# Moving layer 1's closing sums over neighbours beside other small matmuls, and layer 3's loads, in a four-layer graph network

## The chip, the cores and the metric

The kernel runs on one core of a Trainium2 chip. The metric is the device time of one launch in microseconds (us), as the median of several runs. A profile of one further execution gives the order of work on each engine: TensorE (PE, matmuls; PEld is its weight load), VectorE (DVE), ScalarE (ACT), GpSimd (POOL), and SyncE (SP), which here only issues transfers (DMAs).

## The reference

The input is 128 graphs of 64 nodes with 512 features each, an adjacency matrix of 64x64 for each graph, and the weights of four layers. Each layer normalises x over its features, takes the positive part h, and adds a graph operation on h to x. All numbers are 32-bit floats.

```
x = x + softmax_nodes(s * sum(q * (adj @ k)))[:, :, None] * v      # layer 0: q,k,v = h @ W
w = adj * exp(q @ k^T);  x = x + (w / sum(w)) @ v                  # layer 1
x = x + Wo(softmax(scores * 2 adj) @ v)                            # layer 2: 8 heads of 64
a = adj * exp(leaky_relu(sj + si + ab));  t = a / sum(a)           # layer 3
x = x + relu(h@Wk0 + t @ (h@Wk1) + t @ (t @ (h@Wk2)) + biases)
```

## The kernel before

**Tiling.** The 8192 nodes are cut into 32 blocks of 256 (`n_blk` = 32), each of them two groups of 128 rows (`TT` = 2), with two graphs to a group. The large products (512x512 weights) are written by `Product` as seven half-size products of a Strassen-like scheme: `first` and `second` make four of them, `late` the other three, and a `store` helper collects the results from PSUM with ACT, DVE and POOL. `side_by_side` runs the products of two weights together: first and second of part 0, first and second of part 1, late of part 0, late of part 1. It takes three lists of further actions, `between`: list 0 runs after the first part's `first`, list 1 before the late products of part 0, list 2 before those of part 1.

**Small tiles.** Products within a graph have only 64 rows and use a quarter or half of the matrix array. They are: `neighbour_sums` (L390, matmul on L397, 64x64 tiles of the array with 512 columns; its output is called pa in layer 0 and po in layers 1 and 3), den (L601, L861, row sums, one column), `products` (L375, matmul on L382, 128x64 tiles, output sc) and layer 2's scores and context (L665, L731). All other matmuls use the full 128x128 array.

**Order of layers.** Layers 0 and 1 go over pairs of blocks: `steps` (L915) is layer 0 of blocks 0 and 1, layer 1 of blocks 0 and 1, layer 0 of blocks 2 and 3, and so on. Layer 1 of a block ends with `layer1` computing sc and the weights e (L588 to L593). Its end, `layer1_end` (L595: den, po, the division, the addition to x on DVE, and the store of x to DRAM on L613), is put off: the loop keeps it in `open_end` and appends it to list 1 of the next step's `between`, ahead of the late products of that step's first part. Layer 0's end (`layer0_end`, L546, with the matmul sm_w) is put off to list 0 of the next step. `prepare` (L919) loads and normalises the next step's block in list 0, `turned` (L925) transposes it in list 2 (matmul tr, L195). The last end, of block 31, runs in layer 2's first block (L1027).

Layer 2 follows with loads three blocks ahead (`fetch2`), additions and norm in `prepare2` (L935), `layer2_in`, scores, values and context. The output product's `add_to` (L338) collects into x on DVE and POOL and names its last DVE instruction `taken` (L345); `keep_ab` (L281) names its DVE sum `kept` (L286). Layer 3 begins inside layer 2's last blocks: after block 29 and 30 of layer 2 come load, norm and `layer3_dots` (L802, four dot products hu on DVE, L810) of layer 3's blocks 0 and 1. Then `layer3_step(b)` does one block each: `layer3_head` with `begin` (L1003: load and norm of block b+2), the end of block b-1 (`layer3_end`: po, the output and its store on L910), the start of block b+1 (`layer3_in`: sm_i and the transposes); then `layer3_tail`, and last the dots of block b+2.

**Buffers.** PSUM is shared by three pools: `ps_tr` (2 banks, tag tr), `ps_mm` (4 banks, tag mm, two for each `Product`) and `ps_sc` (2 banks, tag sc). A tile has to wait until the earlier user of its bank is done. x has four buffers (`load_x`, L56), used by all layers; adjT has three; h has six.

**What sets the order.** Each engine works through its instructions one after the other. Their order on an engine is settled when the program is built: earlier source lines have precedence, and an instruction from further down is put ahead when the builder takes its inputs to be ready sooner. `tc.issue_after(ins)` holds the instructions of its block that are on the engine of `ins` behind `ins` in that engine's order; it adds no wait for `ins` to finish, and leaves other engines alone. Transfers of x, adjT and outputs are all issued by SP, in SP's order.

Of the kernel before, what the change touches and what calls it, by code (L numbers as in the profile page):

```python
# [13 lines left out]
P = 128  # L14
N = 64
D = 512
# [9 lines left out]
def kernel(ctx: ExitStack, tc: tile.TileContext, a: dict, out: bass.AP):  # L26
# [29 lines left out]
    def load_x(b: int, source, stage: int):  # L56
        x = big.tile([P, TT, D], FP, tag="x", name=f"x{stage}_{b}", bufs=4)
        nc.sync.dma_start(x, tokens(source))
        return x

    def load_adjT(b: int, stage: int):
        adjT = med.tile([P, TT, N], FP, tag="adjT", name=f"adjT{stage}_{b}")
        nc.sync.dma_start(adjT, tokens(adjT_d[rows(b), :]))
        return adjT
# [438 lines left out]
        yield m, u, c1, d, w1v, w2  # L503


    def layer0(b: int, x, adjT, hs, hT, between):
        ops = sums(hT, f"0_{b}")
        gv = big.tile([P, 2, TT, D], FP, tag="qk", name=f"gv_{b}")
        am = small.tile([P, TT, N], FP, tag="am", name=f"am_{b}", bufs=2)
        with tc.issue_after(behind_norm[0][0].ins):  # L510
            nc.gpsimd.tensor_tensor(
                am,
                adjT,
                mcol[:, b * TT : (b + 1) * TT].unsqueeze(2).to_broadcast([P, TT, N]),
                ALU.mult,
            )
        pa = [ps_tr.tile([P, D], FP, tag="tr", name=f"pa_{b}_{t}") for t in range(TT)]
        aggs = [
            med.tile([P, D], FP, tag="agg", name=f"agg_{b}_{t}", bufs=2) for t in range(TT)
        ]  # L520
        for t, to, at in neighbour_sums(pa, am, hs):
            nc.scalar.copy(aggs[t][to], pa[t][at])

        parts = [
            (ops, m0, None, lambda p: p.store(gv[:, 0]), f"g0_{b}"),
            (ops, w0v, None, lambda p: p.store(gv[:, 1]), f"v0_{b}"),
        ]
        side_by_side(*parts[:: 1 if b else -1], between=between)
# [15 lines left out]
        return x, gv, w, wd  # L544
# [21 lines left out]
                x[:, t, :], gv[:, 1, t, :], att[:, t : t + 1], x[:, t, :], ALU.mult, ALU.add  # L566
            )

    def layer1(b: int, x, adjT, hs, hT, between):

        m1, u1, c1, d1, w1v = made1[:5]
        ops = sums(hT, f"1_{b}")
        gT = big.tile([P, K, T], FP, tag="qk", name=f"gT_{b}")
        v = big.tile([P, TT, D], FP, tag="v", name=f"v1_{b}")
        _, of_v = side_by_side(
            (ops, m1, u1, lambda p: p.store_T(gT, u1), f"g1_{b}"),
            (ops, w1v, None, lambda p: p.store(v), f"v1_{b}"),
            between=between,
        )
        be = small.tile([P, TT], FP, tag="be", name=f"be_{b}")  # L580
        for t in range(TT):
            hc = med.tile([P, D], FP, tag="agg", name=f"hc_{b}_{t}", bufs=2)
            with tc.issue_after(of_v.kept.ins):
                nc.vector.scalar_tensor_tensor(
                    hc, hs[t], 1.0, c1, ALU.mult, ALU.mult, accum_out=be[:, t : t + 1]
                )
        nc.vector.tensor_scalar(be, be, d1, None, ALU.add)
        s = products(gT, hT, f"1_{b}")  # L588
        e = small.tile([P, TT, N], FP, tag="e", name=f"e1_{b}")
        for t in range(TT):  # L590
            nc.scalar.activation(e[:, t, :], s[:, t, :], AF.Exp, bias=be[:, t : t + 1])
        nc.vector.tensor_tensor(e, e, adjT, ALU.mult)
        return v, e  # L593

    def layer1_end(b: int, x, v, e, to):  # L595

        po = [ps_sc.tile([P, D], FP, tag="sc", name=f"po1_{b}_{t}") for t in range(TT)]
        den = [ps_tr.tile([P, 1], FP, tag="tr", name=f"den1_{b}_{t}") for t in range(TT)]
        for t in range(TT):
            for g in range(2):  # L600
                nc.tensor.matmul(  # L601
                    den[t][half[g ^ t]], e[half[g], t, :], ones_bd[half[g], g * N : g * N + 1],
                    start=True, stop=True,
                )
        parts = neighbour_sums(po, e, [v[:, t, :] for t in range(TT)])
        r = small.tile([P, TT], FP, tag="r1", name=f"r1_{b}")
        for t in range(TT):
            nc.vector.reciprocal(r[:, t : t + 1], den[t])
        for t, out_at, at in parts:
            nc.vector.scalar_tensor_tensor(  # L610
                x[out_at, t, :], po[t][at], r[at, t : t + 1], x[out_at, t, :], ALU.mult, ALU.add
            )
        nc.sync.dma_start(tokens(to), x)  # L613
# [180 lines left out]
                nc.gpsimd.tensor_tensor(bs, bs, bi, ALU.add)  # L794
        return us, c3, bs

    def layer3_norm(b: int, source):
        x = load_x(b, source, 3)
        adjT = load_adjT(b, 3)
        return x, adjT, norm(x, f"3_{b}")  # L800

    def layer3_dots(b: int, x, adjT, hs):  # L802
# [132 lines left out]
    def prepare2(b: int):  # L935
        if b < n_blk:
# [3 lines left out]
                nc.vector.tensor_tensor(x[:, t, :], x[:, t, :], b1v, ALU.add)  # L940
            normed2[b] = norm(x, f"2_{b}")

    def turned2(b: int):
        if b < n_blk:
            normed2[b] = transposed(normed2[b], f"2_{b}")
# [7 lines left out]
    loaded[1] = load_x(1, x_d[rows(1), :], 0), load_adjT(1, 0)  # L953
    setup = setup1()
    next(setup)
    open_end = []
    for i, (layer, b) in enumerate(steps):
        if i == len(steps) - 2:
            fetch2(0)
        between = [[], [chore], []]  # L960
        if i == 0:
            for n in (1, 2):
                between[n].append(lambda: next(setup))
        if i == 1:
            open_end.clear()
            made1 = next(setup)
        for n, end in open_end:
            between[n].append(end)
        if i + 1 < len(steps):
            between[0].append(lambda: prepare(i + 1))  # L970
            between[2].append(lambda: turned(i + 1))
        else:
            fetch2(1)
            between[0].append(lambda: prepare2(0))
            between[2].append(lambda: turned2(0))
        if layer == 0:
            softmax = layer0(b, *loaded[b], *normed[i], between)
            open_end = [(0, lambda b=b, softmax=softmax: layer0_end(b, *softmax))]
        else:
            attention = layer1(b, *loaded[b], *normed[i], between)  # L980
            open_end = [
                (1, lambda b=b, a=attention: layer1_end(b, loaded[b][0], *a, x1[b]))
            ]
            if b == n_blk - 2:
                open_end.append((1, lambda: fetch2(2)))
        if i == len(steps) - 3:
            made2 = setup2()

# [6 lines left out]
    def layer3_step(b: int, ahead: bool = True):  # L995

        nonlocal normed3
        x, al, ops = made_in.pop(0)  # L1000
        stages = layer3_in(b + 1, *normed3, made_in) if b + 1 < n_blk else iter(())

        def begin():  # L1003
            nonlocal normed3
            if b + 2 < n_blk and ahead:
                normed3 = layer3_norm(b + 2, x2[b + 2])

        y = layer3_head(b, ops, [
            [begin], [ending.pop()], [lambda: next(stages, None), lambda: next(stages, None)]
        ])  # L1010
        yield
        tail = layer3_tail(b, al, ops, y)
        for _ in range(2):
            next(tail)
            yield
        r, y0, kept = next(tail)
        ending.append(lambda: layer3_end(b, x, al, y, r, y0))
        if b + 2 < n_blk:
            with tc.issue_after(kept.ins):
                if ahead:  # L1020
                    normed3 = layer3_dots(b + 2, *normed3)
                else:
                    normed3 = layer3_norm(b + 2, x2[b + 2])
        yield

    qk, ops = layer2_in(0, normed2[0], [
        [lambda: prepare2(1), chore], [*(end for _, end in open_end), chore], [lambda: turned2(1)]  # L1027
    ])
    coming = values(0, ops)
    next(coming)  # L1030
# [8 lines left out]
    for b in range(n_blk):  # L1039
# [43 lines left out]
        if b == n_blk - 4:  # L1083
            made3 = setup3()
        if n_blk - 3 <= b < n_blk - 1:
            normed3 = layer3_dots(
                b - n_blk + 3, *layer3_norm(b - n_blk + 3, x2[b - n_blk + 3])
            )
        elif b == n_blk - 1:
            with tc.issue_after(of_o.taken.ins):  # L1090
                normed3 = layer3_dots(2, *normed3)


    for b in range(1, n_blk):
# [66 lines left out]
```

## Time and profile before

| | |
|---|---|
| median of 3 runs | 2647.34 us (2646.83 to 2647.69) |
| profiled execution: its own time | 2645.07 us |
| profiled execution: span from first to last instruction | 2643.3 us |
| granted TensorE clock, mean | 0.999 |
| TensorE busy | 2624.6 us (99%), 20752 matmuls |
| VectorE busy | 1695.9 us (64%) |
| GpSimd busy | 1292.8 us (49%) |
| ScalarE busy | 950.4 us (36%) |
| den of layer 1 (L601) | 256 matmuls 64x64, 9.3 us |
| po of layer 1 (L397) | 256 matmuls 64x64, 34.2 us |
| sc of layer 1 (L382) | 1024 matmuls 128x64, 36.9 us |
| pa of layer 0 (L397) | 256 matmuls 64x64, 35.9 us |

How to read it: "busy" is the time in which an engine had at least one instruction of the program in work; matmuls overlap in the array, so their durations add up to more than the time they take. In a line such as `L397 PE MATMUL po<-v,e 64*64 64x512 f32 x8`, L397 is the line of the kernel (that of a helper where a helper writes the instruction), `po<-v,e` says what is written from what, `64*64` is the part of the array that is used, and x8 counts instructions. In lines of time the first number is the start in us from the start of the span, the second the duration. "idle before <-X" is idle time of the engine and what ended it. In the view of waits the three numbers are total us, number of waits, and the longest. The chain of work runs back from the last instruction: at each step to what released it.

Layers 0 and 1 take roughly the first 1010 us of the span, layer 2 goes to about 1945 us, layer 3 to the end.

### The profile page before, as it was taken

The page shows a single profiled execution, that of the slowest core. Times are in us where ns is not written, and L with a number is a line of the kernel's source. Part 1 is how long each engine was busy: PE and PEld are TensorE (multiplying, and loading weights), DVE is VectorE, ACT ScalarE, POOL GpSimd, SP SyncE. Part 2 cuts the span into 40 slices and gives each one's busy share as a digit, 9 for nine tenths or more (in the row PEclk, how much of TensorE's full clock was granted, in tenths as well). Part 3 has the DMA queues.
Part 4 walks back from the last instruction along what each step waited for, and adds up shares of the span by engine and source line. Part 5 has one row for each costly group of instructions (what it writes and reads, how often), then busy time and mean ns, then how long its engine had stood idle before and what let it go on. Part 6 is the DMA issues. An engine that isn't in the chain of part 4 may idle for free.

```text
span 2643.3 us, 52749 instructions
## 1 busy us (share of the span) xinstructions
PE 2624.6 (99%) x20752; PEld 2250.6 (85%) x20752; DVE 1695.9 (64%) x4396; ACT 950.4 (36%) x2292; POOL 1292.8 (49%) x1585
## 2 busy tenths in 40 slices
PE   9999999999999999999999999999999999999998
PEld 5888888888888889999999999999877777777776
DVE  5676666666666676556556656656656666666665
ACT  3333343333333343333333333333333333333332
POOL 4443333333433335655655655655565555555554
PEclk9999999999999999999999999999999999999999
DMA  5111111111111122111111111111211111111110
GB/s 179 48 35 35 35 36 37 46 39 43 43 35 35 35 67 79 39 51 40 37 53 38 39 53 37 39 48 42 74 51 52 51 52 52 52 52 51 52 50 32
DMA packets 103200, 129.80 MB, mean 49 GB/s; under 512 B 40870, under 2 KB 50086, under 8 KB 102952
## 3 DMA queue, kind: packets, MB, share of 16 engines
q1 hardware_dynamic: 102376, 125.38, 14.3%
q8 instruction: 163, 2.67, 0.4%
q10 hardware_dynamic: 576, 1.05, 0.1%
q14 instruction: 85, 0.70, 0.1%
HBM read 76.07 MB, written 50.34 MB: 48 GB/s over the span
## 4 chain that ended last, share of the span: by engine, by line
PE 93%; DVE 2%; DMA 2%; POOL 1%; ACT 1%; issue 0%; SPq 0%; ACTq 0%; POOLq 0%; DVEq 0%
PE ab_v L256 12%; PE ab_y L256 11%; PE dc_v L256 9%; PE dc_y L256 8%; PE ab_g L249 4%; PE ab_k L249 4%; PE ab_g L256 4%; PE ab_q L249 4%; PE tr L195 4%; PE ab_o L256 4%; PE dc_g L249 3%; PE dc_g L256 3%; PE po L397 3%; PE dc_k L249 3%; PE dc_q L249 3%; PE dc_o L256 3%
## 5 line engine op out<-in xcount | busy, mean ns | idle before, releaser
L184 ACT ACTIVATE h<-x,nmr,rstd 128x512 f32<-128x512 f32 x256 | 194.4, 806 | 239.8 <-DVE nmr L176 239.8
L174 POOL TENSOR_TENSOR rstd<-ve,neghalf 128x2 f32<-128x2 f32 x128 | 89.6, 700 | 373.8 <-DVE ve L172 373.8
L169 DVE BATCH_NORM_STATS2 stats<-x 128x6 f32<-128x512 f32 x256 | 165.5, 677 | 92.8 <-DMA x<-x 86.7
L256 PE MATMUL ab_y<-L_Wk,hT 128*128 128x256 f32 x768 | 203.9, 388 | 0.1
L256 PE MATMUL ab_v<-L_Wv,hT 128*128 128x256 f32 x768 | 200.8, 384 | 0.4 <-ACT qk L328 0.4
L256 PE MATMUL dc_v<-L_Wv,S 128*128 128x256 f32 x768 | 197.3, 380 | 0.0
L256 PE MATMUL ab_y<-L_Wk,S 128*128 128x256 f32 x768 | 197.2, 379 | 0.0
L256 PE MATMUL ab_v<-L_Wv,S 128*128 128x256 f32 x768 | 197.2, 379 | 0.0
L256 PE MATMUL dc_y<-L_Wk,S 128*128 128x256 f32 x768 | 193.8, 381 | 3.2 <-DVE u_y L882 3.1
L256 PEld LDWEIGHTS ab_y<-L_Wk,hT 128*128 128x128 f32 x768 | 137.3, 190 | 67.5 <-issue 25.2
L256 PEld LDWEIGHTS dc_y<-L_Wk,S 128*128 128x128 f32 x768 | 144.8, 190 | 26.6 <-DVE u_y L882 7.0
L256 PEld LDWEIGHTS ab_v<-L_Wv,S 128*128 128x128 f32 x768 | 146.1, 190 | 19.7
L256 PEld LDWEIGHTS ab_y<-L_Wk,S 128*128 128x128 f32 x768 | 146.1, 190 | 19.7
L256 PEld LDWEIGHTS dc_v<-L_Wv,S 128*128 128x128 f32 x768 | 143.6, 190 | 18.7 <-issue 0.8
L903 POOL TENSOR_TENSOR tz<-tz,y 128x512 f32<-128x512 f32 x63 | 91.3, 1450 | 126.0 <-ACT tz L900 125.9
L256 PEld LDWEIGHTS ab_v<-L_Wv,hT 128*128 128x128 f32 x768 | 136.0, 190 | 16.0 <-ACT qk L328 0.7
L195 PE MATMUL tr<-ident,h 128*128 128x128 f32 x1024 | 133.9, 274 | 0.0
L195 PEld LDWEIGHTS tr<-ident,h 128*128 128x128 f32 x1024 | 118.4, 142 | 7.3
L221 POOL TENSOR_TENSOR S<-hT 128x256 f32<-128x256 f32 x128 | 100.4, 784 | 34.0 <-ACT hT L198 33.6
L224 POOL TENSOR_TENSOR S<-hT 128x256 f32<-128x256 f32 x128 | 107.9, 843 | 7.1 <-DVE hT L200 7.1
L904 DVE SCALAR_TENSOR_TENSOR x<-tz,x 128x512 f32<-128x512 f32 x64 | 44.3, 692 | 102.6 <-POOL tz L903 102.6
L311 POOL TENSOR_TENSOR gv<-u_g,p_g 128x256 f32<-128x256 f32 x32 | 23.3, 729 | 173.0 <-DVE u_g L308 173.0
(238 smaller groups left out, 6474.6 us busy)
## 6 DMA issues: line engine op xcount, KB each, us to landing
x<-x SPq DMA_DIRECT2D x128, 512.0 KB, 3.5
x<-in_x_dram SPq DMA_DIRECT2D x32, 512.0 KB, 3.5
out_dram<-x SPq DMA_DIRECT2D x31, 512.0 KB, 2.8
adjT<-in_adjT_dram SPq DMA_DIRECT2D x64, 64.0 KB, 1.9
adjq<-in_adj_dram SPq DMA_DIRECT2D x64, 64.0 KB, 2.3
L_Wk<-in_L_Wk_dram SPq DMA_DIRECT2D x16, 256.0 KB, 5.5
L_Wv<-in_L_Wv_dram SPq DMA_DIRECT2D x12, 256.0 KB, 4.9
q<-in_L_Wqk_dram ACTq DMA_DIRECT2D x4, 256.0 KB, 5.3
```

What stands on the lines that cost most here:

```text
L169: nc.vector.bn_stats(stats[:, t, :], x[:, t, :])
L174: by_rows = nc.gpsimd.tensor_tensor(rstd, ve, neghalf, ALU.pow)
L184: nc.scalar.activation(h, x[:, t, :], AF.Relu, bias=nmr[:, t : t + 1], scale=rstd[:, t : t + 1])
L195: nc.tensor.transpose(pt[:, k, :], h[:, k * P : (k + 1) * P], ident)
L221: nc.gpsimd.tensor_tensor(S1, A21, A22, ALU.add)
L224: behind[0] = nc.gpsimd.tensor_tensor(S3, A11, A21, ALU.subtract)
L249: nc.tensor.matmul(dst[:, m * P : (m + 1) * P], w[:, place, k, m * P : (m + 1) * P], left[:, k, :], start=key not in self.begun, stop=last ...
L256: nc.tensor.matmul(dst, left[:, k, :], w[:, place, k, :], start=key not in self.begun, stop=last and k == 1, skip_group_check=True,)
L311: nc.gpsimd.tensor_tensor(y[:, 1, F:], self.u3, self.p5, ALU.add)
L397: nc.tensor.matmul(ps[t][half[g ^ t]], e[half[g], t, :], us[t][half[g]], start=True, stop=True)
L903: nc.gpsimd.tensor_tensor(tz[t], tz[t], y0[:, t, :], ALU.add)
L904: nc.vector.scalar_tensor_tensor(x[:, t, :], tz[t], 0.0, x[:, t, :], ALU.max, ALU.add)
```

## The change

Three things change.

1. `layer1_end` of block b no longer goes into a `between` list of the following step. The loop keeps it as the function `open_end`, and `layer0` and `layer1` take it as a new argument `before`, which they call only for odd blocks: `layer1` directly ahead of `products`, `layer0` directly ahead of its `neighbour_sums` (pa). So the end of an even block b runs in layer 1 of block b+1 ahead of sc, and the end of an odd block b in layer 0 of block b+2 ahead of pa. That of block 31 stays where it was. `fetch2(2)` goes along with the end of block 30. To make room, po of layer 1 moves from `ps_sc` to `ps_tr`, den from `ps_tr` to `ps_mm` (for block 31 to `ps_sc`), and pa from `ps_tr` to `ps_sc` (for even blocks one of its two tiles to `ps_mm`; block 0 stays).
2. Layer 3's load of x and adjT is split from its norm into `fetch3`. In `layer3_step(b)` the load of block b+3 is issued at the end of the step, after the dots of b+2; the norm of b+3 stays in `begin` of step b+1.
3. Two parts are tied: `prepare2(0)` behind `kept` of the value product of layer 1's block 30 (`first2`), and `layer3_dots` of blocks 0 and 1 behind `taken` of layer 2's output product.

```diff
-    def layer0(b: int, x, adjT, hs, hT, between):
+    def layer0(b: int, x, adjT, hs, hT, between, before):
...
-        pa = [ps_tr.tile([P, D], FP, tag="tr", name=f"pa_{b}_{t}") for t in range(TT)]
+        before()
+        pa = [
+            pool.tile([P, D], FP, tag=tag, name=f"pa_{b}_{t}")
+            for t, (pool, tag) in enumerate((
+                ((ps_sc, "sc"), (ps_sc if b % 2 else ps_mm, "sc" if b % 2 else "mm"))
+                if b else ((ps_tr, "tr"),) * 2
+            ))
+        ]
...
-    def layer1(b: int, x, adjT, hs, hT, between):
+    def layer1(b: int, x, adjT, hs, hT, between, before):
...
         nc.vector.tensor_scalar(be, be, d1, None, ALU.add)
+        before()
         s = products(gT, hT, f"1_{b}")
...
-        return v, e
+        return of_v, v, e
...
-        po = [ps_sc.tile([P, D], FP, tag="sc", name=f"po1_{b}_{t}") for t in range(TT)]
-        den = [ps_tr.tile([P, 1], FP, tag="tr", name=f"den1_{b}_{t}") for t in range(TT)]
+        po = [ps_tr.tile([P, D], FP, tag="tr", name=f"po1_{b}_{t}") for t in range(TT)]
+        pool, tag = (ps_mm, "mm") if b + 1 < n_blk else (ps_sc, "sc")
+        den = [pool.tile([P, 1], FP, tag=tag, name=f"den1_{b}_{t}") for t in range(TT)]
...
-    def layer3_norm(b: int, source):
-        x = load_x(b, source, 3)
-        adjT = load_adjT(b, 3)
+    loaded3 = {}
+
+    def fetch3(b: int):
+        if b < n_blk:
+            loaded3[b] = load_x(b, x2[b], 3), load_adjT(b, 3)
+
+    def layer3_norm(b: int):
+        x, adjT = loaded3.pop(b)
         return x, adjT, norm(x, f"3_{b}")
...
+    def first2(of_v):
+        with tc.issue_after(of_v.kept.ins):
+            prepare2(0)
+
...
-        for n, end in open_end:
+        for n, end in begun:
             between[n].append(end)
+        begun = []
...
-            between[0].append(lambda: prepare2(0))
+            between[0].append(lambda: first2(of_v))
...
-            softmax = layer0(b, *loaded[b], *normed[i], between)
-            open_end = [(0, lambda b=b, softmax=softmax: layer0_end(b, *softmax))]
+            softmax = layer0(b, *loaded[b], *normed[i], between, open_end if b % 2 else nothing)
+            begun = [(0, lambda b=b, softmax=softmax: layer0_end(b, *softmax))]
         else:
-            attention = layer1(b, *loaded[b], *normed[i], between)
-            open_end = [
-                (1, lambda b=b, a=attention: layer1_end(b, loaded[b][0], *a, x1[b]))
-            ]
-            if b == n_blk - 2:
-                open_end.append((1, lambda: fetch2(2)))
+            of_v, *attention = layer1(
+                b, *loaded[b], *normed[i], between, open_end if b % 2 else nothing
+            )
+
+            def open_end(b=b, a=attention):
+                layer1_end(b, loaded[b][0], *a, x1[b])
+                if b == n_blk - 2:
+                    fetch2(2)
+
...
             if b + 2 < n_blk and ahead:
-                normed3 = layer3_norm(b + 2, x2[b + 2])
+                normed3 = layer3_norm(b + 2)
...
                 if ahead:
                     normed3 = layer3_dots(b + 2, *normed3)
+                    fetch3(b + 3)
                 else:
-                    normed3 = layer3_norm(b + 2, x2[b + 2])
+                    fetch3(b + 2)
+                    normed3 = layer3_norm(b + 2)
...
-            normed3 = layer3_dots(
-                b - n_blk + 3, *layer3_norm(b - n_blk + 3, x2[b - n_blk + 3])
-            )
+            fetch3(b - n_blk + 3)
+            normed3 = layer3_norm(b - n_blk + 3)
+            with tc.issue_after(of_o.taken.ins):
+                normed3 = layer3_dots(b - n_blk + 3, *normed3)
         elif b == n_blk - 1:
             with tc.issue_after(of_o.taken.ins):
                 normed3 = layer3_dots(2, *normed3)
+            fetch3(3)
```

More of the change, by code (lines that the diff above doesn't have):

```diff
@@ L955, with nothing @@
     next(setup)
-    open_end = []
+    begun = []
+    def nothing():
+        pass
+    open_end = nothing
     for i, (layer, b) in enumerate(steps):
@@ L964 @@
         if i == 1:
-            open_end.clear()
+            begun = []
             made1 = next(setup)
-        for n, end in open_end:
+        for n, end in begun:
             between[n].append(end)
+        begun = []
         if i + 1 < len(steps):
@@ L1021, in layer3_step @@
                     normed3 = layer3_dots(b + 2, *normed3)
+                    fetch3(b + 3)
                 else:
-                    normed3 = layer3_norm(b + 2, x2[b + 2])
+                    fetch3(b + 2)
+                    normed3 = layer3_norm(b + 2)
         yield
     qk, ops = layer2_in(0, normed2[0], [
-        [lambda: prepare2(1), chore], [*(end for _, end in open_end), chore], [lambda: turned2(1)]
+        [lambda: prepare2(1), chore], [open_end, chore], [lambda: turned2(1)]
     ])
```

## The prediction, made before the changed kernel was run

> **What bounds the kernel now.** I read the page first (busy times, slices, chain), then the waits of the matrix engine, then the order of time around the moved work, then the chain inside one block of layer 3.
>
> ```profile
> PE 2624.6 (99%) x20752; PEld 2250.6 (85%) x20752; DVE 1695.9 (64%) x4396; ACT 950.4 (36%) x2292; POOL 1292.8 (49%) x1585
> PE 93%; DVE 2%; DMA 2%; POOL 1%; ACT 1%; issue 0%; SPq 0%; ACTq 0%; POOLq 0%; DVEq 0%
> ```
>
> TensorE (PE) is busy 99% of the span and is 93% of the chain that ended last. So time is won only by giving PE fewer or denser instructions, or by ending its few waits:
>
> ```profile
> PE tw_q L424 <- DMA q<-in_L_Wqk_dram: 5.7, 3, 5.1
> PE dc_y L256 <- DVE u_y L882: 3.1, 4, 1.1
> PE ab_o L256 <- DVE u_o L286: 1.5, 1, 1.5
> ```
>
> The first is the start of the kernel and isn't touched. The others lie in layers 2 and 3. Waits are small, so the denser question is what PE does between its matmuls. PE in order of time, in an odd block of layer 1 (start, duration, what):
>
> ```profile
> 516.95 1.03 PE L256 MATMUL dc_v<-L_Wv,hT 128*128 128x256 f32 x4
> 517.91 0.29 PE L601 MATMUL den<-ones_bd,e 64*64 64x1 f32 x8
> 518.05 1.07 PE L397 MATMUL po<-v,e 64*64 64x512 f32 x8
> 519.05 1.16 PE L249 MATMUL ab_g<-hT,fold 128*128 128x128 f32 x8
> 520.04 1.06 PE L249 MATMUL ab_g<-S,fold 128*128 128x128 f32 x8
> 520.93 1.06 PE L249 MATMUL dc_g<-S,fold 128*128 128x128 f32 x8
> ...
> 525.39 1.15 PE L382 MATMUL sc<-hT,gT 128*64 128x64 f32 x32
> 526.47 1.09 PE L397 MATMUL pa<-h,am 64*64 64x512 f32 x8
> 527.49 1.13 PE L256 MATMUL dc_g<-fold,S 128*128 128x256 f32 x4
> ```
>
> Durations overlap, so I take start to start. Four 128x256 matmuls need 0.864 us when more of that kind follow; dc_v takes 0.957 before den (median of the 64x64-bound places): **+0.093 to enter** small tiles. ab_g takes 0.99 after po (519.05 to 520.04), 0.89 otherwise: **+0.104 to leave** (median). den takes 0.137, po 0.998. sc to pa changes small sizes: sc takes 1.082 whether pa or a full product follows, pa 1.019 whether sc or a full product precedes. So neighbours of different small sizes pay neither the 0.093 nor the 0.104 between them.
>
> Inside one block of layer 3 the chain reads:
>
> ```profile
> 2560.87 2.80 DMA out_dram<-x
> 2563.67 0.02 issue
> 2563.68 4.96 DMA x<-x
> 2568.65 0.02 issue
> 2568.67 1.29 DVE stats L169 x2
> ...
> 2573.64 0.42 DVE y L881
> 2574.06 0.34 DVE u_y L882
> 2574.40 0.04 issue
> 2574.45 1.13 PE dc_y L256 x4
> ```
>
> The store of block 27 lands, the load of block 31 starts 0.02 us later into the freed buffer, bn_stats waits for it at the head of VectorE's (DVE's) queue, the sums L872 to L882 stand behind it, and PE waits for L882.
>
> **What the Trainium skill says.** "TensorEngine Tiling (Array Packing)", Key Properties: "Changing tiling mode (not just tile) drains the TensorE". The trace agrees: 0.093 and 0.104 around each run of small tiles, 0.038 from den to po in the same size. "Perfetto Trace Analysis", Tensor Engine Instruction: matmul ends are computed by the profiler, and DVE, ACT and GpSimd are strict first-in first-out. Hence I count from starts; the trace shows the queueing above. "DMA: Bandwidth & Descriptors", Anatomy of one DMA: a transfer's semaphore wait is done by the issuing sequencer; so SP stands still, as at 2563.67. "PSUM — Partial Sum Buffer", Specifications: 8 banks per partition. The pools hold 2+4+2 banks, so po and den can only move by borrowing another user's bank; no row shows banks.
>
> **The change, part by part.**
>
> *1. layer1_end next to other small tiles.* 31 of 32 ends move (b=31 stays inside layer 2's first block). Before, each costs 0.093+0.137+0.998+0.104 = 1.332.
> Even b (16): den, po, then sc. The end adds 0.137+0.998 = 1.135 there, since entry and exit are sc's anyway: 0.197 saved. po to sc (64x64 to 128x64) isn't in the trace, only the reverse. Bounds: nothing saved if it drained like two full switches; 0.277 if it cost as little as one size (0.080 less: the last matmul of a po run stands 0.519 before a full product, 0.439 before its like). I take the reverse's price: 16 x 0.197 = 3.15 (0 to 4.4).
> Odd b (15): den, po, then pa, all 64x64. po shrinks by 0.519-0.439 = 0.080 to about 0.92, pa by 0.02 (0.46 against 0.44 between its halves): it adds 0.137+0.92-0.02 = 1.04, so 0.294 saved, 15 x 0.294 = 4.41 (2.9 to 4.4).
> Sum **-7.56**.
> What waits instead? DVE has two reciprocals (0.23) and three scalings (2.28) per end, now later. Odd b: at 541.95 DVE does wd and the three store operations to 543.84, is idle to 545.25, and gets 1.04 more before sm_w; 1.41+1.04 = 2.45 against 2.51, and the chain to the transposes has 0.6 to spare (h done 552.60, its second half needed at 553.26). ScalarE's (ACT's) copies of pa (2.9 us after pa starts) must free a ps_sc bank before sm_w, also 2.9 after: the first copy is done at 1.7, enough if that bank is taken. Even b: DVE ends its stores 1.0 after sc's start and pa's first product comes after 3.2. den borrows ps_mm banks; the next dc_g needs one 2.1 us (odd) or 3.2 us (even) after den begins: in the odd case the four banks are free at about -2.5 (those den takes), +1.0, +1.9, and den's own at +2.0. Nothing waits; I charge 0.
> SP: the store of x1 (L613) comes up to 8.5 us later, and the x load that waits for its landing too (540.92 becomes about 549.5); adjT behind it likewise. Their stats run from 563 on, am for pa 10 us after its adjT: hidden. fetch2(2), two DMAs, moves along with the store; block 2 of layer 2 is some 40 us off. POOL's am (0.40) waits in a gap of over 7 us: 0.
>
> *2. The two ties.* first2 holds L940 and the norm behind an earlier DVE instruction. Before, L940 stood at 966.13 waiting 0.77 for its x, delayed the sums behind it, and PE lost 0.153+0.103 at 971: **-0.26**. What then stands behind the tied ones on DVE is layer 2's, with gaps of 1.8 and 3.1 us at 1011 and 1015.
> layer3_dots(0) and (1) go behind of_o.taken. Before, one dot (0.97) ran at 1891.60 ahead of u_o L286, whose input was ready at 1891.50; PE lost 1.63+0.10 there. Without it L286 ends about 0.9 sooner: -0.85. The four dots no longer delay L342 to L345, so x2's store and the next x come about 1.8 sooner, and the wait of 0.58+0.10 at 1909 (bn_stats waits 3.40 for x) goes: -0.68. The dots (about 4.5 us with di, sj) now end near 1901.2; sm_i is due at about 1902: tight, up to +0.5 if late. Sum **-1.5** (-1.8 to 0).
>
> *3. fetch3.* The load of x3 for b+3 moves in the source from the start of step b+1 to the end of step b, with no engine's order tied. But SP already issues it in step b's head, bound by the buffer: 0.02 us after the store lands. It can't start sooner with four buffers, and norm keeps its place. So **0**, although 11 waits of PE for it from 1980 on sum to 5.57 (start-to-start excess over 1.727 per eight 128x256). Bounds: -5.6 if norm is reordered so that it no longer blocks, +2 if transfers fall worse (loads took 3.7 to 5.0 us; from about 3.9 on PE pays).
>
> Sum: -7.56-0.26-1.53 = -9.35. The profiled execution took 2645.07 (span 2643.3 and 1.8 around it), the median is 2647.34, 2.27 more; the edits are the same work in both, so 2647.34-9.35 = **2638.0**.
>
> **Rivals.**
> A, likeliest (0.54): as summed, 2638.0, own range 2636 to 2640.
> B (0.17): fetch3 or its side effects do end layer 3's waits: 2638.0-5.2 = 2632.8. For: the waits are there, 83.3 us of DVE's time. Against: the chain shows a buffer, not an issue too late.
> C (0.14): the builder puts ready small tiles where PE looks idle, or po to sc drains in full: even b saves nothing, the ties half: 2638.0+3.15+0.9 = 2642.0, spread 2640 to 2645.
> D (0.07): the change doesn't bring den and po beside sc and pa, or new short waits take it all: 2647.
> E (0.08), slower: den's reciprocals stand behind wd and the stores on DVE while den holds a ps_mm bank that the next dc_g is given. Place: first product after pa, 31 times. It decides from 9.35/31 = 0.30 us per place; at 0.5 us, 15.5-9.35 = +6.2: 2653.5. Against: two other banks are free by then; for: den's own margin is under 0.1.
>
> **Numbers.** 0.2% is 5.3 us, about what a measurement tells from no change. Faster by more: A, B, half of C: 0.78. Within: half of C, most of D: 0.13. Slower: E and a little of D: 0.09. The range takes B below and C above: 2631.5 to 2644.0.
>
> **What would show it.** den, po, sc (or pa) adjacent, with 0.957 once before den and 0.104 once after the last; 31 fewer drains. No wait of dc_g for a reciprocal. No hu ahead of u_o L286. bn_stats L169 in layer 3 still waiting some 83 us for x. I am wrong if den still stands between full products, if PE's waits in layers 0 and 1 pass 1 us, or if the waits of dc_y for L882 are gone.

## The result, and the profile after

The changed kernel takes 2640.77 us (median of 17 runs, 2638.48 to 2641.76) against 2646.73 us of the kernel before measured beside it (2643.82 to 2648.78): ratio 0.9979, 95% interval 0.9972 to 0.9985, which is 5.96 us or some 0.2% less. The profiled execution took 2639.59 us (span 2637.8). In the page of the changed kernel the first line is busy time, the second the shares of the chain that ended last; then a row of the costliest groups, with idle time before it and what ended most of that:

```profile
PE 2618.6 (99%) x20752; PEld 2253.9 (85%) x20752; DVE 1696.3 (64%) x4396; ACT 951.3 (36%) x2292; POOL 1294.2 (49%) x1585
PE 94%; DVE 3%; DMA 2%; POOL 1%; ACT 1%; issue 0%; ACTq 0%; POOLq 0%; SPq 0%; DVEq 0%
...
L169 DVE BATCH_NORM_STATS2 stats<-x 128x6 f32<-128x512 f32 x256 | 165.2, 676 | 91.4 <-DMA x<-x 85.0
```

TensorE is busy 6.0 us less for the same 20752 matmuls, so they lie closer together. bn_stats still waits 85 us for x (86.7 before): moving the load in the source did not end that. The waits of TensorE in the changed kernel (total, times, longest):

```profile
PE tw_q L424 <- DMA q<-in_L_Wqk_dram: 5.7, 4, 4.7
PE tr L195 <- ACT h L184: 1.7, 1, 1.7
PE dc_y L256 <- DVE u_y L896: 1.6, 3, 0.8
...
PE ab_o L256 <- DVE u_o L286: 0.6, 1, 0.6
...
PE ab_g L249 <- DVE u_g L286: 0.3, 1, 0.3
PE sm_i L405 <- DVE di L829: 0.3, 1, 0.3
```

The rows of tr, ab_g and sm_i are new. The wait for u_o fell from 1.5 to 0.6. L896 is the old L882. Then TensorE in order of time (start, duration), around the end of an even and of an odd block:

```profile
520.96 1.03 PE L256 MATMUL dc_v<-L_Wv,S 128*128 128x256 f32 x4
521.91 0.29 PE L610 MATMUL den<-ones_bd,e 64*64 64x1 f32 x8
522.05 1.07 PE L397 MATMUL po<-v,e 64*64 64x512 f32 x8
523.05 1.15 PE L382 MATMUL sc<-hT,gT 128*64 128x64 f32 x32
524.13 1.09 PE L397 MATMUL pa<-h,am 64*64 64x512 f32 x8
525.15 1.13 PE L256 MATMUL dc_g<-fold,S 128*128 128x256 f32 x4
...
537.35 1.03 PE L256 MATMUL dc_v<-L_Wv,S 128*128 128x256 f32 x4
538.31 0.29 PE L610 MATMUL den<-ones_bd,e 64*64 64x1 f32 x8
538.45 1.07 PE L397 MATMUL po<-v,e 64*64 64x512 f32 x8
539.34 1.04 PE L397 MATMUL pa<-h,am 64*64 64x512 f32 x8
540.30 1.13 PE L256 MATMUL dc_g<-fold,S 128*128 128x256 f32 x4
```

Start to start, medians over all blocks: even, den 0.137, po 0.998, sc 1.082, as taken. Odd, po 0.888 and pa 0.968, less than taken (0.92 and 1.00). The lines on both sides of the moved work before the change are in the prediction. The seams give 16 x 0.197 = 3.15 and 15 x 0.358 = 5.37 us, together **8.5**.

Where the rest of it went is read by stages. I cut every trace at the same four matmuls: the first pa of block 1 (after the last setup matmul pf, L440), layer 2's first dc_q, the first pu (layer 3's weights, inside layer 2's last blocks), and the last matmul of layer 2's output product. The column of layer 3 runs from there to the start of the last matmul of all. Each row's stages are from one execution; the ratio is that of the medians, each against the kernel before measured beside it. The middle of layer 2 takes 852.9 to 853.0 in all of them and is left out.

How far one execution can be trusted differs by stage. The changed kernel, 7, 9 and 10 have the same layers 0 and 1 and lie within 0.14 us there, before and 3 within 0.2. Before, 1, 2, 4 and 5 have the same layer 3, and these five executions reach from 678.2 to 680.3: loads of x that take over about 3.9 us make TensorE wait there, and which loads these are changes from one execution to the next. So 0.4 us is a finding in layers 0 and 1, and 2 us is none in layer 3.

| kernel | start | layers 0 and 1 | end of layer 2 | layer 3 | ratio to before, interval |
|---|---|---|---|---|---|
| before | 60.5 | 947.98 | 94.16 | 680.28 | 1 |
| changed | 61.9 | 942.26 | 94.30 | 678.66 | 0.9979 (0.9972-0.9985) |
| 1 even ends only | 62.3 | 965.72 | 94.30 | 679.57 | 1.0076 (1.0062-1.0089) |
| 2 odd ends only | 61.4 | 944.68 | 94.19 | 678.22 | 0.9979 (0.9972-0.9986) |
| 3 loads only | 61.0 | 948.16 | 94.18 | 680.04 | 1.0000 (0.9992-1.0009) |
| 4 ties only | 61.4 | 948.10 | 94.13 | 679.98 | 1.0006 (0.9997-1.0014) |
| 5 even ends, pa's banks moved | 61.9 | 945.58 | 94.15 | 680.01 | 0.9994 (0.9986-1.0002) |
| 6 changed + block 1's preparation held | 62.5 | 939.48 | 94.56 | 679.06 | 0.9973 (0.9964-0.9982) |
| 7 changed + layer 3's norm held | 61.8 | 942.20 | 94.16 | 679.84 | 0.9982 (0.9976-0.9989) |
| 8 both of these | 62.2 | 939.49 | 94.37 | 680.03 | 0.9972 (0.9962-0.9982) |
| 9 changed + norm held, behind tz too | 61.5 | 942.30 | 94.46 | 675.38 | 0.9964 (0.9952-0.9977) |
| 10 changed + dots held behind u_o | 62.1 | 942.34 | 97.36 | 679.84 | 0.9994 (0.9986-1.0003) |
| 11 = 6 + 9 + 10 | 62.0 | 939.44 | 97.04 | 675.28 | 0.9969 (0.9957-0.9980) |
| 12 = 6 + 9 | 61.9 | 939.57 | 94.96 | 675.98 | 0.9952 (0.9938-0.9965) |

In the changed kernel layers 0 and 1 won 5.72, not 8.5. The missing 2.8 us are new waits, the largest at 967 us. Its trace there, TensorE, DVE, ACT and SP (in brackets idle time and what ended it):

```profile
960.30 0.37 SPq L622 DMA_DIRECT2D x<-x  x1
963.16 1.28 DVE L169 BATCH_NORM_STATS2 stats<-x 128x6 f32<-128x512 f32 x2
963.34 0.36 SPq L58 DMA_DIRECT2D x<-x  x1
...
966.92 1.03 PE L256 MATMUL dc_g<-fold,S 128*128 128x256 f32 x4
966.96 0.69 DVE L954 TENSOR_TENSOR x<-x,L_bv 128x512 f32<-128x512 f32 x1 [2.04 <-DMA x<-x]
967.57 0.16 DVE L172 TENSOR_SCALAR ve<-mv 128x2 f32<-128x2 f32 x1
...
968.74 1.52 ACT L184 ACTIVATE h<-x,nmr,rstd 128x512 f32<-128x512 f32 x2 [2.90 <-DVE nmr L176]
969.61 1.36 PE L195 MATMUL tr<-ident,h 128*128 128x128 f32 x8 [1.66 <-ACT h L184]
```

Block 29's store (L622) lands, layer 2's x of block 1 is loaded, and DVE stands idle for 2.04 us until it lands, at L954, an addition that was ordered between the statistics and L172 of **block 30's norm**. That norm, h and the transposes tr wait with it; TensorE loses 1.82 + 0.33 = 2.15. The other new waits are 0.30 near 97, 0.54 near 994, and 0.09 and 0.05 in two more places, in all 3.1; the 0.26 that TensorE lost near 971 before is gone. In the kernel before, the same load, addition and statistics stood so:

```profile
962.52 0.36 SPq L58 DMA_DIRECT2D x<-x  x1
...
966.13 1.29 DVE L940 TENSOR_TENSOR x<-x,L_bv 128x512 f32<-128x512 f32 x2 [0.77 <-DMA x<-x]
...
970.19 1.28 DVE L169 BATCH_NORM_STATS2 stats<-x 128x6 f32<-128x512 f32 x2
```

The load was issued 7.7 us ahead of block 30's statistics; now it comes 0.2 us after their start. And the addition stood ahead of the norm, not inside it.

### The profile page after: what moved, and what is told of

Its sections match the earlier page's. It is cut to its first block, busy times and chain, and to the rows that moved or that the text cites. A ratio compares the mean times of both kernels' runs of the same rounds, so it can differ in the third digit from the quotient of the medians.

```text
span 2637.8 us, 52811 instructions
## 1 busy us (share of the span) xinstructions
PE 2618.6 (99%) x20752; PEld 2253.9 (85%) x20752; DVE 1696.3 (64%) x4396; ACT 951.3 (36%) x2292; POOL 1294.2 (49%) x1585
## 4 chain that ended last, share of the span: by engine, by line
PE 94%; DVE 3%; DMA 2%; POOL 1%; ACT 1%; issue 0%; ACTq 0%; POOLq 0%; SPq 0%; DVEq 0%
PE ab_v L256 12%; PE ab_y L256 11%; PE dc_v L256 9%; PE dc_y L256 8%; PE ab_g L249 4%; PE ab_k L249 4%; PE ab_q L249 4%; PE tr L195 4%; PE ab_o L256 4%; PE ab_g L256 4%; PE dc_g L249 3%; PE po L397 3%; PE dc_g L256 3%; PE dc_k L249 3%; PE dc_q L249 3%; PE dc_o L256 3%
## 5 line engine op out<-in xcount | busy, mean ns | idle before, releaser
L918 DVE SCALAR_TENSOR_TENSOR x<-tz,x 128x512 f32<-128x512 f32 x64 | 44.2, 691 | 103.3 <-POOL tz L917 103.2
L222 POOL TENSOR_TENSOR S<-S,hT 128x256 f32<-128x256 f32 x128 | 102.3, 799 | 11.4 <-DVE ve L172 9.8
```

The lines of the kernel that those rows point to most:

```text
L222: nc.gpsimd.tensor_tensor(S2, S1, A11, ALU.subtract)
L918: nc.vector.scalar_tensor_tensor(x[:, t, :], tz[t], 0.0, x[:, t, :], ALU.max, ALU.add)
```

## The experiments

Experiments 1 to 5 start from the kernel before, 6 to 12 from the changed one.

**1. Even ends only.** `before()` is called in `layer1` and not in `layer0`; odd ends stay in list 1 with their old banks, and pa keeps its old ones.

```diff
+        before()
         s = products(gT, hT, f"1_{b}")
...
-        po = [ps_sc.tile([P, D], FP, tag="sc", name=f"po1_{b}_{t}") for t in range(TT)]
+        pool, tag = (ps_sc, "sc") if b % 2 else (ps_tr, "tr")
+        po = [pool.tile([P, D], FP, tag=tag, name=f"po1_{b}_{t}") for t in range(TT)]
...
```

> The kernel before, with only the ends of even blocks moved ahead of sc (16 of the 31; odd ends, the loads and the ties as before). Theory (each small-tile run that joins another saves its own way in and out, 0.093 + 0.104): 16 x 0.197 = 3.15 us less, no new wait on TensorE over 0.3 us, so -3.1 (ratio 0.9988). Rival (going from 64x64 to 128x64 tiles drains the array like two full switches, and the gain is all in the odd ends): 0 to -0.5. Rival (the gain comes from the loads or the ties): 0.

It came out 0.76% slower, which no theory of mine had. Its trace (TensorE and DVE) shows a cause that I had overlooked when I left pa's banks alone:

```profile
534.46 1.07 PE L397 MATMUL po<-v,e 64*64 64x512 f32 x8
535.56 2.30 DVE L616 SCALAR_TENSOR_TENSOR x<-po,r,x 128x512 f32<-128x512 f32 x3 [0.17 <-PE po L397]
536.54 1.07 PE L397 MATMUL pa<-h,am 64*64 64x512 f32 x4
537.91 1.07 PE L397 MATMUL pa<-h,am 64*64 64x512 f32 x4 [0.30 <-DVE x L616]
```

pa of the next block follows sc and needs the two ps_tr banks that po has just filled; DVE's three scalings free them late, and pa takes 2.38 instead of 1.02 us: 1.36 lost, or 1.16 when the seam's gain is taken off. 15 x 1.36 = 20.4 lost, 3.15 won: +17.3 of the +17.7 in that stage. This is rival E's mechanism (a bank held by DVE's closing work), at another bank: without the moves of pa to ps_sc and ps_mm the even ends would lose time. Experiment 5 is the test of this.

**2. Odd ends only**, with pa's banks as in the change; the even ends go back to list 1 with their old banks:

```diff
+        if layer == 1 and b % 2:
+            between[1].append(open_end)
+            open_end = nothing
```

> The kernel before, with only the ends of odd blocks moved ahead of pa, and pa's banks changed as in the change (15 ends; even ends, the loads and the ties as before). Theory: the seams save 15 x 0.358 = 5.4 us by the trace of the changed kernel (4.41 in the prediction), but the store of block 29's x comes later, layer 2's first addition for block 1 (L954) is ordered into the middle of block 30's norm on VectorE and waits there some 2 us for its load, which costs TensorE about 2.1, where the kernel before lost 0.26: -5.4 + 1.9 = -3.5. The same wait at about 967 us must show, although no tie is in this kernel. Rival (the tie of layer 2's block 0 pushed that addition forward): no such wait, and -5.4. Rival (the loads or the ties give the gain): 0.

Layers 0 and 1: -3.30, as expected. The same wait stands in this kernel, without any tie:

```profile
969.14 0.69 DVE L954 TENSOR_TENSOR x<-x,L_bv 128x512 f32<-128x512 f32 x1 [1.99 <-DMA x<-x]
...
971.78 1.36 PE L195 MATMUL tr<-ident,h 128*128 128x128 f32 x8 [1.69 <-ACT h L184]
```

So the tie is not the cause; the wait comes with the odd ends. They brought two things here, block 29's later store with the load behind it, and the new place of L954 in DVE's order. Which of the two weighs more is not separated. The medians' -5.24 is 1.9 us more than the stage has. In the profiled execution as much lies in layer 3 (678.22 against 680.28), which this kernel leaves untouched, so it can be chance there; why the medians of 18 and 38 runs differ by more than the stage is not shown.

**3. Loads only** (fetch3 as in the change, nothing else), and **4. Ties only** (`first2`, and the dots of blocks 0 and 1 behind `taken`):

```diff
# 3
...
+                    fetch3(b + 3)
...
# 4
-            between[0].append(lambda: prepare2(0))
+            between[0].append(lambda: first2(of_v))
...
+            with tc.issue_after(of_o.taken.ins):
+                normed3 = layer3_dots(b - n_blk + 3, *normed3)
```

> The kernel before, with only layer 3's load split from its norm and put at the end of the step before. Theory: the load is bound by its buffer, the norm keeps its place on VectorE, so 0 (-0.5 to +0.5); bn_stats in layer 3 waits 83 to 94 us for x and dc_y waits for L882's successor some 4 to 5.6 us in all, as before. Rival (the 1.5 us that layer 3 became shorter in the changed kernel is the loads' doing): -1.5. Rival B of the prediction: -5.

> The kernel before, with only the two ties (layer 2's first preparation, and the dot products of layer 3's blocks 0 and 1). Theory: the first tie holds block 0's addition, but the addition that made TensorE wait 0.26 near 971 us is block 1's, which isn't tied: 0. The dots no longer stand ahead of u_o: -0.9, but sm_i and what follows it come late by about 0.6 to 1.1: net -0.3 to +0.3. Prediction: -1.5. A gain of over 1 us would say that the ties work as predicted and that something else took the gain back in the changed kernel.

Neither differs measurably from before: 1.0000 and 1.0006, every stage after the start within 0.3 us. So fetch3 gives nothing that can be seen, and the ties are not the -1.5 predicted. The 1.6 us by which layer 3 is shorter in the changed kernel is no work of the loads: without fetch3 the stage took 678.2 to 680.3 (five executions, mean 679.6), with it and the norm where it was 678.7 to 680.0 (four: changed, 3, 6 and 10, mean 679.4). The trace also shows that the edit moves no load. In layer 3 the load of x is issued 19.96 us (median) after the den ahead of it, before, in 3 and in the changed kernel alike. What a load that really starts sooner would do was therefore not tested.

**5. Even ends only, with pa of even blocks in a ps_sc and a ps_mm bank.**

```diff
-        pa = [ps_tr.tile([P, D], FP, tag="tr", name=f"pa_{b}_{t}") for t in range(TT)]
+                ((ps_sc, "sc"), (ps_mm, "mm")) if b and b % 2 == 0 else ((ps_tr, "tr"),) * 2
```

> As the first kernel with only even ends moved, but pa of even blocks goes to a ps_sc and a ps_mm bank as in the change, so that it no longer needs the ps_tr banks of the po that now stands just ahead of it. Theory (the 1.16 us per pair of blocks that the first one lost is pa waiting for these banks): the waits of pa for the additions to x go, and the seams give 16 x 0.197 = 3.15; layers 0 and 1 take 947.98 - 3.15 = 944.8 us from the first pa of block 1 to layer 2, ratio 0.9988. Rival (po ahead of sc costs time itself, banks or not): layers 0 and 1 stay above 948.

pa's waits are gone, and layers 0 and 1 win 2.40, far more than the 0.2 by which this stage varies; the medians alone could not tell it from nothing. By places: the seams win 3.15, and new waits lose 0.28 at 97 us, 0.41 at 970 (beyond the 0.26 of before) and 0.07 at two others. The seam from 64x64 to 128x64 is as free of the 0.093 and the 0.104 as the reverse; rival C is out.

**6. Changed kernel, layer 2's preparation of block 1 held too**, behind the kept sum of block 31's value product:

```diff
-        [lambda: prepare2(1), chore], [open_end, chore], [lambda: turned2(1)]
+        [lambda: first2(of_v, 1), chore], [open_end, chore], [lambda: turned2(1)]
```

> The changed kernel, with layer 2's preparation of block 1 held on VectorE behind the last kept sum of layer 1's block 31, so that its additions can't stand in the norm of block 30 and wait there for their load. Theory: the waits of dc_g and tr near 967 to 971 us go (2.15 us), perhaps also 0.5 near 994; layers 0 and 1 take 942.26 - 2.15 = 940.1 us (939.6 with the rest), in all 2.2 to 2.7 less than the changed kernel. Rival (VectorE's wait there only shows where TensorE would have lost the time anyway): 942 or more, with a new wait in its place.

939.48: 2.78 less. The waits of dc_g and tr (2.15), that near 995 (0.54) and the small one near 981 (0.09) are all gone. So these three come from the place of block 1's additions and norm on DVE, given the moment of their load.

**7. Changed kernel, layer 3's norm held behind the last DVE instruction of the tail**, and **8. the holds of 6 and 7 together:**

```diff
-                normed3 = layer3_norm(b + 2)
+                with tc.issue_after(tails[-1].ins):
+                    normed3 = layer3_norm(b + 2)
...
+        tails.append(kept)
```

> The changed kernel, with layer 3's norm of block b+3 held on VectorE behind the last instruction of the tail of block b, so that bn_stats no longer waits for x ahead of the sums that TensorE needs. Theory (these waits are TensorE's only ones in layer 3, and the order on VectorE is their cause, not the moment of the load): dc_y waits for u_y go, about 3.7 us in the changed kernel; layer 3 from the end of layer 2 takes 678.66 - 3.7 = 675.0 us. Rival (the norm then comes too late for the dots and transposes of the same block): waits of tr or sm_i instead, 678 or more.

> The changed kernel with both of these holds, layer 2's preparation of block 1 and layer 3's norm. Theory: the two gains are in different stages and add up, -2.2 to -2.7 and -3.7: about 6 us less than the changed kernel, 12 less than the kernel before, ratio 0.9955. Rival (one of the holds only moves a wait): 0.997 or more.

The rival won in 7, with another wait than it named. bn_stats waits only 8.0 us for x and the waits of dc_y for L896 are gone, yet layer 3 takes 679.84. In 29 places ab_y now starts late, in 27 of them by some 0.05, and takes another 0.104: 5.0 us in all. ScalarE and DVE around one of them (TensorE's ab_y starts at 2339.24, when u_y L308 is done):

```profile
2332.30 1.52 ACT L184 ACTIVATE h<-x,nmr,rstd 128x512 f32<-128x512 f32 x2 [3.40 <-DVE nmr L176]
...
2334.24 2.10 ACT L914 ACTIVATE tz<-po,r 128x512 f32<-128x512 f32 x3
...
2338.16 0.69 DVE L918 SCALAR_TENSOR_TENSOR x<-tz,x 128x512 f32<-128x512 f32 x1 [1.16 <-POOL tz L917]
2338.77 0.42 DVE L308 TENSOR_TENSOR u_y<-ab_y,p_y 128x256 f32<-128x256 f32 x1
```

The norm's two activations h stand ahead of tz on ScalarE, tz is late, so are POOL's tz and DVE's additions to x (L918), and the sum u_y L308 is queued behind these. In 8 the first hold gave its 2.8, the second nothing.

**9. The same hold, with the norm after `layer3_end` in list 1, and its activations held behind tz on ScalarE:**

```diff
-            [begin], [ending.pop()], [lambda: next(stages, None), lambda: next(stages, None)]
+            [], [ending.pop(), begin], [lambda: next(stages, None), lambda: next(stages, None)]
...
+                with tc.issue_after(tails[-1].ins), tc.issue_after(scaled3[-1].ins):
+                    normed3 = layer3_norm(b + 2)
```

> The changed kernel, with layer 3's norm of block b+3 placed after the end of the block before (list 1), on VectorE behind the last instruction of the tail, and on ScalarE behind the scalings tz (L914). Theory (in the first hold of this norm the long waits for x went, but the norm's two activations h, 1.52 us, stood ahead of tz on ScalarE, so that POOL's tz and VectorE's last addition to x came late, and u_y L308 and ab_y behind them: 28 times about 0.15 us): with h behind tz both kinds of wait go, and layer 3 from the end of layer 2 takes 678.66 - 3.7 = 675 us. Rival (VectorE has no room for the norm at this place, whatever stands on ScalarE): the 0.15 per block stays, 678 or more.

675.38, within 0.4 of the expectation; both kinds of wait are all but gone. The place in list 1 and the hold behind tz were changed together, so how much each does is not separated. The page's row of bn_stats:

```profile
L169 DVE BATCH_NORM_STATS2 stats<-x 128x6 f32<-128x512 f32 x256 | 164.8, 674 | 14.0 <-DMA x<-x 8.5
```

One place of layer 3, first in the changed kernel, then in this one:

```profile
2344.89 1.29 DVE L169 BATCH_NORM_STATS2 stats<-x 128x6 f32<-128x512 f32 x2 [3.35 <-DMA x<-x]
...
2349.53 0.41 DVE L896 TENSOR_TENSOR u_y<-ab_y,p_y 128x256 f32<-128x256 f32 x1
...
2349.99 0.48 PE L256 MATMUL dc_y<-L_Wk,S 128*128 128x256 f32 x1 [0.28 <-DVE u_y L896]
```

```profile
2344.08 0.41 DVE L896 TENSOR_TENSOR u_y<-ab_y,p_y 128x256 f32<-128x256 f32 x1
...
2348.92 1.27 DVE L169 BATCH_NORM_STATS2 stats<-x 128x6 f32<-128x512 f32 x2
```

bn_stats now comes after L896, and starts without a wait. Layer 3's waits were a matter of DVE's order: bn_stats starts 6.7 us later after den (8.71 against 1.99, medians), while the load is issued only 0.6 us sooner (19.40 against 19.96).

**10. Changed kernel, dots held behind `kept` (u_o) instead of `taken`.**

```diff
-            with tc.issue_after(of_o.taken.ins):
+            with tc.issue_after(of_o.kept.ins):
                 normed3 = layer3_dots(b - n_blk + 3, *normed3)
```

> The changed kernel, with the dot products of layer 3's blocks 0 and 1 held behind u_o L286 (the sum that TensorE waits for) instead of behind the last sum of the output product. Theory (the hold itself wins 0.9 at dc_o, and being held as far back as the last sum loses 0.55 at sm_i): the wait of dc_o stays at 0.73, those of dc_k, sm_i and ab_q near 1897 go, and the end of layer 2 (from pu to the last output product) takes 94.3 - 0.5 = 93.8 us. Rival (the dots then delay the store of x2 and the load behind it, and layer 2's last blocks wait for that): 94.3 or more.

The waits near 1897 went, as expected, but the stage is 3.06 longer, as the rival said. SP, DVE and TensorE in this kernel:

```profile
1896.74 0.37 SPq L1111 DMA_DIRECT2D x<-x  x1
...
1901.56 0.37 SPq L58 DMA_DIRECT2D x<-x  x1
...
1905.26 0.69 DVE L169 BATCH_NORM_STATS2 stats<-x 128x6 f32<-128x512 f32 x1 [5.93 <-DMA x<-x]
...
1907.85 2.07 PE L256 MATMUL ab_v<-L_Wv,hT 128*128 128x256 f32 x4 [3.39 <-ACT qk L328]
```

The store of x2 is issued about 0.5 us later than in the changed kernel (counted from the same dc_o), but it takes 4.8 us to land instead of 2.7; load and bn_stats follow, with layer 2's sums behind them. So the dots' own delay, which the rival named, is the smaller part. The DMA packets of the trace show the larger: 1.8 us after the store's issue a 16 KB packet of the queue called "instruction" begins, and takes 0.93 us. By 2.4 us all but 16 of the store's 256 packets of 2 KB are through; these follow one after the other, from the end of that packet (2.7) to 4.35. In 11, where the store took 4.4, such a packet of 1.48 us lies inside it in the same way; in the changed kernel it comes 3.4 us after the store's issue, when the store has landed. Why the packet falls just there is not shown.

**11** and **12** join the pieces:

> The changed kernel with layer 2's preparation of block 1 held, layer 3's norm placed as in the kernel that holds it behind tz, and the dots held behind u_o. Theory: the gains lie in three stages and add up, -2.8 -3.7 -0.5: about 7 us less than the changed kernel, 13 less than the kernel before, ratio 0.9952. Rival (waits move on between the stages): ratio 0.997 or more.

> The changed kernel with layer 2's preparation of block 1 held and layer 3's norm placed behind the tail and tz, and with the dots held as in the change (the hold behind u_o cost 3 us at the end of layer 2). Theory: layers 0 and 1 take 939.4 us, the end of layer 2 94.4, layer 3 675.3; 6.1 us less than the changed kernel, about 12 less than the kernel before, ratio 0.9955. Rival (the two holds disturb each other): 0.997 or more.

11 keeps the loss of 10. 12, without it, is the fastest: 2633.88 us against 2646.57 beside it, 12.7 us less, where the changed kernel has 6.0 less; the two intervals don't meet. Between the two profiled executions it is 10.6.

## Why the prediction was right and wrong

The time, 2640.8, lies in the range, and faster by 0.2% was the likelier side; the measured gain is just above 0.2%, and its interval (0.15 to 0.28%) holds both sides. The range is wide, and the hit owes something to it: 2640.8 lies outside case A's own range (2636 to 2640) and inside that of case C, whose mechanism experiment 5 rules out. A's seams are the right mechanism; its sum of -9.35 was 3.4 us too much against the medians (-5.96) and 3.9 against the traces' spans (-5.5). One of the named signs of being wrong came true: TensorE's new waits in layers 0 and 1 pass 1 us. By its own steps:

- **Even seams, -3.15:** right to the hundredth by the seam's medians; experiment 5 agrees, once its new waits are counted.
- **Odd seams, -4.41:** -5.37. The mis-sized term is the last po matmul before pa: I took 0.439 (as inside a po run), it is 0.409; and pa shrinks by 0.05, not 0.02, since both its halves now take 0.41. Together 0.358 per block instead of 0.294.
- **"Nothing waits; I charge 0":** this failed, by 3.1 us (2.86 net of the 0.26 that went). The step "their stats run from 563 on: hidden" followed the later store only to layer 0's next x. At the last pair the same store is ahead of layer 2's x of block 1, whose addition now has a place on DVE in the middle of block 30's norm: 2.15 (experiments 2 and 6). And I looked for waits at the place to which den and po went, not at the one they left: at 97 and 994 us they had given u_g time to be done, and without them ab_g loses 0.30 and 0.54. The one at 994 also needs ScalarE's h of block 1 there, since experiment 6 removes it.
- **Borrowed banks, rival E:** no dc_g waits for a reciprocal, as I worked out. Experiment 1 shows what the even ends cost without the move of pa: 1.36 us a pair. The prediction did not price it.
- **first2, -0.26:** wrong instruction. L940 at 966.13 belongs to block 1, and the tie holds block 0's: experiment 4, with the tie, keeps that wait (0.43), and experiment 6, which holds block 1's, ends it. The view gives no block numbers; I assumed the nearest source line.
- **Dots, -0.85 and -0.68, "+0.5 if late":** the first was 0.90. The lateness came, 0.43 + 0.07 + 0.05 = 0.55 at sm_i. The second failed: the wait near 1904 is still there (0.75 after 0.58). I had x2's store bound by L345 on DVE; it is bound by POOL. In the changed kernel:

```profile
1891.01 0.41 DVE L345 TENSOR_TENSOR x<-dc_o,x 128x256 f32<-128x256 f32 x1
1891.24 2.49 POOL L708 TENSOR_TENSOR e<-e,r 128x512 f32<-128x512 f32 x2
...
1893.69 1.17 POOL L346 TENSOR_TENSOR x<-u_o,x 128x256 f32<-128x256 f32 x1
1894.83 1.17 POOL L347 TENSOR_TENSOR x<-u_o,x 128x256 f32<-128x256 f32 x1
...
1896.02 0.37 SPq L1111 DMA_DIRECT2D x<-x  x1
```

  L345 ends 3 us sooner than before (against dc_o), the store is issued only 0.5 sooner. POOL's work from L340 to L347 takes 6.1 to 6.2 us in both kernels: L708 stands ahead of the last sums, and the two sums that run beside the dots take 1.17 each, L340 and L341 before, L346 and L347 now. With a new wait of dc_y of 0.33 near 1927 the end of layer 2 is +0.14 instead of -1.53.
- **fetch3, 0:** right (experiment 3), and for one of the two stated reasons: bn_stats kept its place (85 us of waiting after, 87 before). The other, a load bound by its buffer 0.02 us after the store lands, was read from one block and holds in 2 of the 20 whose landing is on the trace. In the other 18 the load starts 0.53 to 0.88 us after the landing, because SP issues the block's adjT first and stands waiting for a DVE instruction there. Neither the buffer nor this queue was changed by fetch3. Experiment 9 shows that the bound of -5.6 "if norm is reordered" was of the right kind: 3.3 us.

The bridge: -9.35 - 0.96 (odd seams) + 3.1 (waits in layers 0 and 1) + 1.67 (dots) = -5.5, with the chance differences of start and layer 3 (+1.4 and -1.6) nearly cancelling. That they cancel is luck, and so is part of the closeness: the better odd seams hid a third of the waits.

"TensorEngine Tiling (Array Packing)", Key Properties, of the Trainium skill says that a change of tiling mode drains the array. The runs agree where full products stand on both sides, and add a price: 0.093 + 0.104. Between po and sc, which changes the mode too, neither of the two is paid; only the last po stands 0.519 ahead of sc, as it does ahead of a full product, against 0.409 ahead of pa, which keeps po's mode. The 0.104 is not peculiar to a change of mode: the same 0.104 follows where TensorE has waited for a sum, as behind the waits near 97 and 994.

## What to carry to other kernels

Price a regrouping of instructions from start-to-start times at its seams, which was right to the hundredth here where the seam's like stood in the trace; then look for new waits at the place that the work left (whose cover was it?) and down every queue whose releases moved (a store, then the load behind it, then the first instruction that reads it, and what is queued behind that, at the last iteration and the next stage too). A load that stands sooner in the source need not start sooner: see what it waits for, in the buffer and in its queue, in more than one block. Here it was the reader, at the head of DVE's queue, that had to move, with a look at each engine on which it has instructions. When tiles get new neighbours, look at the PSUM banks they share: the wait for a bank cost 1.36 us where the seam gave 0.197. Layer 3's waits also change from one execution to the next, so a gain there is believed only beyond that spread.

## What the runs showed of the hardware that I had not expected

Eight po matmuls of 64x512 directly followed by pa's run closer than before anything else: the last stands 0.409 us ahead of pa, against 0.439 between the halves of po and 0.519 ahead of sc or a full product. A start that is only 0.05 us late costs TensorE another 0.104 in the following 128x256 group (experiment 7). Of POOL's last 128x256 sums into x (L346, L347) in the changed kernel, five of the six beside DVE's dot products took 1.17 us, the others 0.72 to 0.76; the dots in turn took 0.68 us without a POOL addition beside them and 1.20 with one (medians). The same store of 512 KB took 2.7 us in one kernel and 4.8 in another whose edit concerns only DVE's order; a 16 KB packet of the instruction queue fell into the second. Over the 14 traces 461 stores of x without such a packet in their time took 2.78 us (median, nine in ten under 2.93), 106 with one 3.51 (one in ten 4.7 or more).
